# Which stream takes its turn first in a three-stage batch pipeline

## The chip, the cores and the metric

The kernel runs on one core of a Trainium2 chip. Times are device microseconds (us) of one execution. The core has a matrix engine (PE, with weight loads shown apart as PEld), a vector engine (DVE), an activation engine (ACT), a small-program engine (POOL) and a queue that issues DMA transfers (SP). Each engine works through its own instructions in the order in which they stand in its queue, and waits on semaphores for the others.

## The reference

Four graph layers run over x of shape (16, 1024, 128), 16 batches of 1024 nodes, with one 0/1 adjacency matrix of 1024 x 1024 for each batch. Every layer adds its result to x and norms each row. Layer 0 is a gated graph attention:

```
h = x @ W_w.T + W_b
e = einsum('bjl,bkl->bjk', h @ A, h);  e = e + swapaxes(e, 1, 2)
att = softmax(where(adj > 0, e, -9e15), axis=1) * adj
h_prime = relu(att @ h)
coeff = sigmoid(concat[x, h_prime] @ gate_w.T + gate_b)
x = layernorm(x + coeff * x + (1 - coeff) * h_prime)
```

Layer 1 thins the adjacency row after row (a sequential rule) and runs three graph convolutions with batch norms over all batches. Layer 2 is an attention of the same kind as layer 0 with three gates, a sigmoid and a tanh. Layer 3 is a graph convolution: two elus over x @ W0, then twice "multiply by a 128 x 128 matrix, propagate along the normed adjacency, add a bias", with an elu between, and the last residual and norm.

## The kernel before, in words

Nodes are tiled by 128, so a batch has NT = 8 tiles. The program has three stages that matter here: layer 0; layer 1 (thinning and convolutions); and layers 2 and 3 together. Layer 0 and layers 2 and 3 are each written as three Python generators over one batch, and the helper `in_turn` runs them as a pipeline.

`before(s, b)` prepares a batch. In layer 0 it loads x and eight adjacency blocks (L891, L895), casts each block on ACT (L897), tests it on DVE (L900), turns it on PE (L904) and stores it as fp8 (L905), and between them makes hT, G and hn, the attention's operands (L907 to L926). In layers 2 and 3 it loads the stored adjacency, three hidden matrices and x (L1208 to L1215), multiplies the hidden matrices by Wl (L765), adds, norms the rows, and makes hT, G and hn.

`attention(s, b)` goes over eight tiles and yields after each. For a tile it writes an additive mask on ACT (L939, L1554), multiplies the scores on PE (L723, in two halves of 512 columns), adds the mask and takes the row maximum on DVE (L942, L1559), takes the exponential on ACT (L946, L1563), forms scaled rows hs on DVE (L950, L1570) and accumulates on PE into `acc` (L953, L1573). The score tiles have two PSUM buffers and `acc` one.

`after(s, b)` ends a batch. It reads `acc` through a relu into hpT (L959, L1579), multiplies the gates on PE with 1 or 3 columns (L962, L1584), mixes x and h on DVE and norms the rows. In layers 2 and 3 the whole of layer 3 follows: turned rows x3T (L1613), the U0 product, two elus (L1481 to L1487), products with U1 and U2 (L1496), two propagations of 64 half-size matmuls in all (L1510), a last residual and norm, and the store of the output. Short PE products of all streams share two PSUM buffers with the tag `h`.

The row norm `normed` (L771 to L784) is the same everywhere: statistics on DVE (L777, L779), one add on DVE (L741), a power on POOL (L744), a product on DVE (L782) and eight scalings on ACT (L784). In the queue of DVE, L782 waits for POOL, and whatever stands behind it waits too.

What sets the order: `take_turns` steps through a list of streams and takes one yield from each in turn, and `in_turn` makes that list. The order of the Python calls is a priority. The framework's planner then fills each engine's queue: among the instructions whose inputs and buffers it expects to be free, it takes the one that was called first. So an engine's order is not the written order, and a turn that comes earlier in the list wins where two streams have something ready at once.

Of the kernel before, what the change touches and what calls it, by code (L numbers as in the profile page):

```python
# [639 lines left out]
def fast_kernel(ctx: ExitStack, tc: tile.TileContext, t: dict, out: bass.AP, flag: bass.AP):  # L640
# [45 lines left out]
    def nat(ap):  # L686
        return ap.rearrange("(t p) d -> p t d", p=P)
# [32 lines left out]
    def wide_matmul(psum, lhsT, rhs, tag="w"):  # L720
        p = psum.tile([P, N], F32, name="pmm", tag=tag)
        for h in range(H2):
            nc.tensor.matmul(p[:, h * 512:(h + 1) * 512], lhsT, rhs[:, h * 512:(h + 1) * 512],  # L723
                             start=True, stop=True)
        return p

    def tiles3(ap):
        return ap.rearrange("p (t d) -> p t d", d=P)

    def per_row(v):  # L730

        return v[:, :, None].to_broadcast([P, NT, P])
# [20 lines left out]
    def turned(psum, src, tag="h"):  # L753

        for p, c, blocks in halves(psum, tag):
            for i, k in enumerate(blocks):
                s = src[:, k, :] if len(src.shape) == 3 else src[:, k * P:(k + 1) * P]
                nc.tensor.transpose(p[:, i * P:(i + 1) * P], s, identf)  # L758
            yield p, c, slice(blocks[0], blocks[-1] + 1)
# [8 lines left out]
    def half_rows(v):  # L768

        return v[:, :, None].to_broadcast([P, 4, P])  # L770

    def normed(small, r):

        st = small.tile([P, NT, 6], F32, name="ln_st")
        mv = small.tile([P, NT, 2], F32, name="ln_mv")
        for i in range(NT):
            nc.vector.bn_stats(st[:, i, :], r[:, i, :])  # L777
        for i in range(NT):
            nc.vector.bn_aggr(mv[:, i, :], st[:, i, :])  # L779
        rstd = power_mhalf(small, mv[:, :, 1], add=LN_EPS, name="ln_rstd")  # L780
        nb = small.tile([P, NT], F32, name="ln_nb")
        nc.vector.scalar_tensor_tensor(nb, mv[:, :, 0], -1.0, rstd, op0=OP.mult, op1=OP.mult)  # L782
        for i in range(NT):
            nc.scalar.activation(r[:, i, :], r[:, i, :], AF.Identity, scale=rstd[:, i:i + 1], bias=nb[:, i:i + 1])  # L784
# [4 lines left out]
    def take_turns(streams):  # L789
        while streams:  # L790
            streams = [s for s in streams if next(s, streams) is not streams]

    def in_turn(before, attention, after, ahead=1, state=None):

        state = state or [Batch() for _ in range(B)]
        take_turns([before(state[b], b) for b in range(ahead)])
        for b in range(B - 1):
            streams = [attention(state[b], b)]  # L800
            if b:
                streams.append(after(state[b - 1], b - 1))
            if b + 1 >= ahead:
                streams.append(before(state[b + 1], b + 1))
            take_turns(streams)
        last, beside = attention(state[B - 1], B - 1), after(state[B - 2], B - 2)
        for i, _ in enumerate(last):
            if i % 2:
                next(beside, None)
        take_turns([beside, after(state[B - 1], B - 1)])  # L810
# [56 lines left out]
    with ExitStack() as ph:  # L867
# [62 lines left out]
        def attention(s, b):  # L930


            s.acc = ps_a.tile([P, N], F32, name="acc")
            for jt in range(NT):
                js = slice(jt * P, (jt + 1) * P)
                c = b * NT + jt
                mx = mx0[:, c:c + 1]
                msk = work.tile([P, N], BF16, name="msk", bufs=2)
                nc.scalar.activation(msk, Y[b][:, jt, :], AF.Identity, scale=BIG, bias=nbig)  # L939
                e = wide_matmul(ps_w, s.hT[:, js], s.G)  # L940
                em = work.tile([P, N], F32, name="em", bufs=2)
                nc.vector.tensor_tensor_reduce(em, e, msk, 1.0, -3.0e38, op0=OP.add, op1=OP.max, accum_out=mx)  # L942
                nmx = small.tile([P, 1], F32, name="nmx")
                nc.vector.tensor_scalar(nmx, mx, -1.0, None, op0=OP.mult)
                sm = small.tile([P, 1], F32, name="sm")
                nc.scalar.activation(em, em, AF.Exp, bias=nmx, accum_out=sm)  # L946
                rs = small.tile([P, 1], F32, name="rs")
                nc.vector.reciprocal(rs, sm)
                hs = small.tile([P, P], F32, name="hs")
                nc.vector.tensor_scalar(hs, s.hn[:, js], rs, None, op0=OP.mult)  # L950
                for h in range(H2):
                    c = slice(h * 512, (h + 1) * 512)
                    nc.tensor.matmul(s.acc[:, c], hs, em[:, c], start=(jt == 0), stop=(jt == NT - 1))  # L953
                yield

        def after(s, b):

            hpT = work.tile([P, N], F32, name="hpT")
            nc.scalar.activation(hpT, s.acc, AF.Relu)  # L959
            pz = ps_h.tile([P, NT], F32, name="pz", tag="h")  # L960
            for i in range(NT):
                nc.tensor.matmul(pz[:, i:i + 1], hpT[:, i * P:(i + 1) * P], gw[:, 1:2], start=True, stop=True)  # L962
            co = small.tile([P, NT], F32, name="co")
            nc.vector.tensor_add(co, pz, s.gx)
            nc.scalar.activation(co, co, AF.Tanh, scale=0.5, bias=gbh)
            cx = small.tile([P, NT], F32, name="cx")
            nc.vector.tensor_scalar(cx, co, 0.5, 1.5, op0=OP.mult, op1=OP.add)
            nc.vector.tensor_scalar(co, co, -0.5, 0.5, op0=OP.mult, op1=OP.add)
            yield
            r = work.tile([P, NT, P], F32, name="r")  # L970
            nc.vector.tensor_mul(s.xn, s.xn, per_row(cx))
            for p, c, k in turned(ps_h, hpT):
                nc.vector.tensor_mul(r[:, k, :], tiles3(p), half_rows(co[:, k]))
            nc.vector.tensor_add(s.xn, s.xn, r)
            yield
            normed(small, s.xn)
            nc.gpsimd.dma_start(nat(x1_d[b]), s.xn)
            yield

        in_turn(before, attention, after)  # L980


# [7 lines left out]
    with ExitStack() as ph:  # L990
# [171 lines left out]
        for i in range(len(steps) + 1):  # L1162
            streams = [fixed_point(*steps[i])] if i < len(steps) else []
# [58 lines left out]
    with ExitStack() as ph:  # L1222
# [194 lines left out]
        for l in range(3):  # L1417
# [9 lines left out]
            for i in range(B + lag[l]):  # L1427
                streams, left = left, []
# [31 lines left out]
    with ExitStack() as ph:  # L1460
# [115 lines left out]
        def after(s, b):  # L1576
# [64 lines left out]
            yield  # L1641

        in_turn(before, attention, after, 2, l2.state)
    l2.ctx.close()

# [45 lines left out]
```

## Time and profile before

| | us |
|---|---|
| median of 9 runs | 3121.43 |
| lowest and highest | 3108.71, 3126.36 |
| the profiled execution | 3126.31 |
| its span, from first to last instruction | 3124.6 |
| mean granted PE clock in it | 0.961 |
| first preparation of layer 0, alone | 0 to about 82 |
| layer 0, batches in the pipeline | 82 to 745 (PE busy 630.6, DVE 553.1, ACT 497.2) |
| thinning | 745 to about 1150 |
| convolutions of layer 1 and the first preparations of layer 2 | about 1150 to 1968 |
| layers 2 and 3, batches in the pipeline | 1968 to 3046 (PE busy 1008.3, DVE 738.0, ACT 698.4) |
| the last batch's end | 3046 to 3124.6 |

The profile is of one execution. Busy time is the union of an engine's instructions, and matmuls overlap at their ends. A row of a timeline has the start in us from the first instruction, the length, the engine, the line of the kernel, the operation, what it writes and reads, the shape, and how many equal instructions follow each other; brackets hold the idle time before it and what ended it. PE makes two passes over a 32-bit matmul, so one such matmul in the code is two in the profile. The granted clock is the share of PE's full clock that the chip let it have.

### The profile page before, as it was taken

How to read it: one execution, taken by the hardware profiler on the slowest of the kernel's cores; microseconds unless marked ns; L12 is line 12 of the kernel's file. 1: busy time of each engine (PE TensorE's matmuls, PEld its weight loads, DVE VectorE, ACT ScalarE, POOL GpSimd, SP SyncE). 2: the span in 40 equal slices, each digit the busy share in tenths (PEclk: the TensorE clock that was granted, in tenths of full speed). 3: DMA queues.
4: the chain of work that ended last, by engine and by line, in shares of the span. 5: the costliest groups of instructions: out<-in, count | busy, mean ns of one | idle time of the engine just before them, and what ended most of it. 6: DMA issues, size and time to landing. Idle time of an engine off the chain costs nothing.

```text
span 3124.6 us, 43145 instructions
## 1 busy us (share of the span) xinstructions
PE 2861.8 (92%) x15379; PEld 1846.8 (59%) x15442; DVE 2331.8 (75%) x5971; ACT 2017.5 (65%) x3393; POOL 326.8 (10%) x292
## 2 busy tenths in 40 slices
PE   7999999996899988999999987999999999999996
PEld 4454545453566655777788873555555555555554
DVE  7888888886999985666688785676666666766665
ACT  5777777774788775565555534666666666666653
POOL 0000000003000001111112231001000001100000
PEclk9999999998999999999999998999999999999997
DMA  5344434430000005223367692112111111111000
GB/s 173 130 138 149 136 132 145 145 125 29 1 2 2 2 25 211 82 95 122 122 220 247 220 346 74 35 61 68 65 57 54 62 67 55 54 55 54 21 14 22
DMA packets 123216, 297.98 MB, mean 95 GB/s; under 512 B 12656, under 2 KB 64624, under 8 KB 115824
## 3 DMA queue, kind: packets, MB, share of 16 engines
q1 hardware_dynamic: 102384, 211.13, 20.7%
q0 software_dynamic: 20608, 84.00, 7.1%
q8 instruction: 124, 2.03, 0.3%
q14 instruction: 100, 0.82, 0.1%
HBM read 211.04 MB, written 84.02 MB: 94 GB/s over the span
## 4 chain that ended last, share of the span: by engine, by line
PE 57%; DVE 22%; issue 5%; ACT 4%; POOL 4%; DMA 2%; POOLq 0%; SPq 0%; DVEq 0%; ACTq 0%
PE acc L1269 9%; PE ph L1510 7%; PE pmm L723 7%; PE acc L1573 5%; PE acc L953 4%; PE ph L765 4%; PE ph L758 4%; PE ph L1373 3%; PE s L1128 3%; POOL ln_rstd L744 3%; DVE ln_st L777 2%; PE ph L1496 2%; DVE mid L1082 2%; PE acc L1246 1%; DVE keep L1132 1%
## 5 line engine op out<-in xcount | busy, mean ns | idle before, releaser
L723 PE MATMUL pmm<-G,hT 128*128 128x512 f32 x1024 | 509.2, 619 | 6.8 <-DVE mx L942 3.4
L723 PEld LDWEIGHTS pmm<-G,hT 128*128 128x128 f32 x1024 | 186.3, 198 | 182.5 <-issue 138.9
L784 ACT ACTIVATE xn<-xn,ln_nb,ln_rstd 128x128 f32<-128x128 f32 x512 | 209.1, 481 | 121.2 <-DVE ln_nb L782 121.1
L1573 PE MATMUL acc<-em,hs 128*128 128x512 f32 x512 | 247.3, 598 | 22.1 <-DVE hs L1570 20.5
L953 PE MATMUL acc<-em,hs 128*128 128x512 f32 x512 | 254.3, 622 | 11.6 <-DVE hs L950 8.7
L744 POOL TENSOR_TENSOR ln_rstd<-ln_rstd,mhalf 128x8 f32<-128x8 f32 x64 | 117.0, 1828 | 1384.7 <-DVE ln_rstd L741 1063.3
L1269 PE MATMUL acc<-a,lo 128*128 128x512 f32 x768 | 241.1, 398 | 2.0 <-DVE lo L1237 2.0
L1269 PE MATMUL acc<-a,hi 128*128 128x512 f32 x768 | 242.1, 399 | 0.6 <-ACT a L1258 0.4
L1130 ACT ACTIVATE q<-s,negc 128x512 f16<-128x512 f32 x256 | 170.3, 693 | 66.9 <-issue 29.3
L1128 PE MATMUL s<-step,carry 128*128 128x384 bf16 (+3 forms) x1035 | 200.6, 305 | 7.3 <-DVE carry L1098 3.2
L1559 DVE CUSTOM_DVE_ANT_0 em<-pmm,msk 128x1024 f32<-128x1024 f32 x128 | 155.7, 1217 | 67.6 <-PE pmm L723 44.8
L1142 ACT ACTIVATE carry<-pc,negone 128x512 fp8e4<-128x512 f32 x256 | 166.4, 693 | 40.0 <-PE pc L1141 30.1
L939 ACT ACTIVATE msk<-carry,l0nbig 128x1024 bf16<-128x1024 fp8e4 x128 | 145.3, 1141 | 64.1 <-DVE mx L942 49.0
L900 DVE SCALAR_TENSOR_TENSOR chk<-an 128x1024 fp8e4<-128x1024 f32 x128 | 156.2, 1220 | 32.7 <-DMA an<-in_adj 31.8
L897 ACT ACTIVATE ab<-an 128x1024 bf16<-128x1024 f32 x128 | 134.6, 1052 | 69.9 <-PE pt L904 42.4
L942 DVE CUSTOM_DVE_ANT_0 em<-pmm,msk 128x1024 f32<-128x1024 f32 x128 | 155.6, 1215 | 24.6 <-PE acc L953 19.2
L1269 PEld LDWEIGHTS acc<-a,lo 128*128 128x128 f32 x768 | 142.8, 188 | 42.8 <-DVE lo L1237 9.5
L905 DVE TENSOR_SCALAR carry<-pt 128x1024 fp8e4<-128x1024 bf16 x128 | 155.2, 1217 | 16.4 <-PE pt L904 16.2
L953 PEld LDWEIGHTS acc<-em,hs 128*128 128x128 f32 x512 | 93.6, 196 | 122.4 <-issue 94.8
L1554 ACT ACTIVATE msk<-A,nbig 128x1024 bf16<-128x1024 fp8e4 x128 | 145.5, 1138 | 31.0 <-DVE mx L1559 28.7
L1573 PEld LDWEIGHTS acc<-em,hs 128*128 128x128 f32 x512 | 92.5, 190 | 117.1 <-issue 79.4
L1269 PEld LDWEIGHTS acc<-a,hi 128*128 128x128 f32 x768 | 141.6, 188 | 33.5 <-ACT a L1258 1.1
(278 smaller groups left out, 6601.4 us busy)
## 6 DMA issues: line engine op xcount, KB each, us to landing
an<-in_adj SPq DMA_DIRECT2D x128, 512.0 KB, 3.5
adj_d<-carry POOLq DMA_DIRECT2D x16, 1024.0 KB, 4.9
A<-dil_d SPq DMA_DIRECT2D x16, 1024.0 KB, 6.3
rdeg<-rdeg_d SPq DMA_DIRECT2D x32, 512.0 KB, 4.2
ag_d<-ag POOLq DMA_DIRECT2D x32, 512.0 KB, 5.3
ag<-ag_d SPq DMA_DIRECT2D x32, 512.0 KB, 6.2
A<-adj_d SPq DMA_DIRECT2D x16, 1024.0 KB, 4.9
xn<-in_x SPq DMA_DIRECT2D x16, 512.0 KB, 3.8
```

The lines of the kernel that those rows point to most:

```text
L723: nc.tensor.matmul(p[:, h * 512:(h + 1) * 512], lhsT, rhs[:, h * 512:(h + 1) * 512], start=True, stop=True)
L744: nc.gpsimd.tensor_tensor(r, r, mhalf[:, :n], op=OP.pow)
L784: nc.scalar.activation(r[:, i, :], r[:, i, :], AF.Identity, scale=rstd[:, i:i + 1], bias=nb[:, i:i + 1])
L900: nc.vector.scalar_tensor_tensor(chk, an, 0.0, an, op0=OP.is_gt, op1=OP.not_equal, accum_out=other[:, c:c + 1], saturate=False)
L953: nc.tensor.matmul(s.acc[:, c], hs, em[:, c], start=(jt == 0), stop=(jt == NT - 1))
L1128: nc.tensor.matmul(s[:, lo or 0:], y, twos if lo is None else step[:, :512 - lo], start=(j == 0), stop=(j == len(terms) - 1))
L1130: nc.scalar.activation(q[:, h * 512:(h + 1) * 512], s, AF.Abs, bias=st.negc[:, i:i + 1])
L1142: nc.scalar.activation(Y[b][:, hb, ks], pc, AF.Relu, bias=negone, saturate=False)
L1269: nc.tensor.matmul(acc, part[:, jt, :], pieces[h * NT // 2 + i][:, j, :], start=(jt == 0 and p == 0), stop=(jt == NT - 1 and p == 1))
L1510: nc.tensor.matmul(p, part[:, jt, :], A[:, jt, c], start=(jt == 0 and i == 0), stop=(jt == NT - 1 and i == 1))
L1559: nc.vector.tensor_tensor_reduce(em, e, msk, 1.0, 0.0, op0=OP.add, op1=OP.max, accum_out=mx)
L1573: nc.tensor.matmul(s.acc[:, c], hs, em[:, c], start=(jt == 0), stop=(jt == NT - 1))
```

## The change

`in_turn` makes its list of streams in another order. Before, the attention of batch b comes first, then the end of batch b - 1, then the preparation of the next batch. After, the end of batch b - 1 comes first, the attention of batch b second, the preparation third. The first round has no ending batch, and the last two steps after the loop are not touched. `in_turn` is called once in layer 0 (preparing one batch ahead) and once for layers 2 and 3 (two ahead).

```diff
         for b in range(B - 1):
-            streams = [attention(state[b], b)]
+            streams = []
             if b:
                 streams.append(after(state[b - 1], b - 1))
+            streams.append(attention(state[b], b))
             if b + 1 >= ahead:
                 streams.append(before(state[b + 1], b + 1))
             take_turns(streams)
```

## The prediction

> **What bounds the kernel now.** I read the totals first.
>
> ```profile
> PE 2861.8 (92%) x15379; PEld 1846.8 (59%) x15442; DVE 2331.8 (75%) x5971; ACT 2017.5 (65%) x3393; POOL 326.8 (10%) x292
> ```
>
> PE is nearly full on the mean, so only PE's gaps in the two stages that the edit touches can be won or lost. Layer 0 runs from 82 to 745 us, layers 2 and 3 from about 1968 to 3046. Next I took the engines' busy time batch by batch, a batch running from one gate matmul (L962 or L1584) to the next. Columns: window, its length, PE, PEld, DVE, ACT and POOL busy, granted clock, DMA share, GB/s. The first line is a batch of layer 0, the others are three successive batches of layers 2 and 3.
>
> ```profile
> 310.49:354.93 44.44, 41.12 (x189) 21.98 (x188) 38.52 (x93) 32.57 (x54) 3.16 (x3) 1.00 0.43 142
> 2178.31:2249.89 71.58, 66.60 (x267) 40.64 (x266) 50.63 (x156) 47.86 (x94) 6.75 (x4) 1.00 0.18 59
> 2249.89:2324.84 74.95, 69.96 (x267) 42.87 (x266) 50.63 (x156) 48.19 (x94) 6.75 (x4) 0.95 0.17 57
> 2324.84:2401.95 77.11, 72.53 (x267) 45.23 (x266) 50.67 (x156) 48.34 (x94) 6.75 (x4) 0.91 0.17 55
> ```
>
> At full clock a batch of layers 2 and 3 takes 71.6 us, with 5.0 us of PE gap each time; the longer batches are the same work under a lower clock. Where the 5.0 us are, the timeline of PE shows (start, length, instruction, in brackets the gap before and what ended it), in another full-clock batch, which starts at 2700.53:
>
> ```profile
> 2722.83 3.60 PE L723 MATMUL pmm<-G,hT 128*128 128x512 f32 x8
> 2728.01 1.12 PE L1573 MATMUL acc<-em,hs 128*128 128x512 f32 x2 [1.58 <-DVE hs L1570]
> ...
> 2732.24 1.88 PE L765 MATMUL ph<-x3T,U 128*128 128x512 f32 x4
> 2733.96 1.02 PE L723 MATMUL pmm<-G,hT 128*128 128x512 f32 x2
> 2737.90 2.22 PE L1496 MATMUL ph<-U,ehi 128*128 128x128 f32 x16 [2.92 <-DVE ehi L1483]
> ...
> 2741.00 0.63 PE L758 MATMUL ph<-identf,xn 128*128 128x128 f32 x4 [0.43 <-DVE zn L1498]
> ```
>
> The 2.92 us is the ending batch's elu chain (L1485 to L1483), with one half score tile (L723, 0.86 us) beside it. The 1.58 us is a DVE queue that stands behind a layer norm; DVE's and POOL's timelines:
>
> ```profile
> 2724.83 1.20 DVE L1526 TENSOR_TENSOR xn<-xn,yn 128x1024 f32<-128x1024 f32 x1
> 2727.59 0.17 DVE L782 SCALAR_TENSOR_TENSOR ln_nb<-ln_mv,ln_rstd 128x8 f32<-128x8 f32 x1 [1.55 <-POOL ln_rstd L744]
> 2727.67 0.28 DVE L1570 TENSOR_SCALAR hs<-hn,rs 128x128 f32<-128x128 f32 x1
> ```
>
> ```profile
> 2725.00 2.55 POOL L744 TENSOR_TENSOR ln_rstd<-ln_rstd,mhalf 128x8 f32<-128x8 f32 x1 [14.70 <-DVE rs L1568]
> 2731.45 1.64 POOL L744 TENSOR_TENSOR ln_rstd<-ln_rstd,mhalf 128x8 f32<-128x8 f32 x1 [3.90 <-DVE nmx L1561]
> ```
>
> In layer 0 PE's gaps are smaller and scattered, each a buffer or a scale that DVE hands over late:
>
> ```profile
> 326.14 1.98 PE L723 MATMUL pmm<-G,hT 128*128 128x512 f32 x4 [0.53 <-DVE mx L942]
> ...
> 333.47 1.95 PE L953 MATMUL acc<-em,hs 128*128 128x512 f32 x4 [0.92 <-DVE hs L950]
> ...
> 338.89 1.13 PE L765 MATMUL ph<-hT,l0As 128*128 128x512 f32 x2 [0.87 <-DVE carry L905]
> ```
>
> **The change, part by part.** No instruction is added or removed on any engine, and the three norm calls and every DMA stay. The turn decides which instruction the planner takes first when several are ready, so the edit acts in the 14 rounds with all three streams (b = 1 to 14), twice: 28 batches. The sums below follow the planned order of the changed kernel by hand: each queue in order, an instruction starting when its engine, its inputs and its buffer are there, durations from the rows. Times below count from the batch's first gate matmul.
>
> *Layers 2 and 3.* Full-size PE matmuls cost 0.43 us per pass, two passes for a half tile (0.86). PE work of a batch, passes times rows: scores, accumulations and projections 88 x 0.43 = 37.8; transposes 48 x 0.109 = 5.2; U products 32 x 0.1125 = 3.6; gates 3.6; propagation 64 x 0.2265 = 14.5; sum 64.8. Against 71.6, 6.8 us are lost: 4.9 in the three gaps, the rest in waits below a gap (0.58 and 0.55 inside runs of transposes).
>
> (a) *The 2.92 us.* In the new order an accumulation half and five score halves, 6 x 0.86 = 5.2 us, stand between the U0 product and L1496 (before: one). The chain gets longer, since an exp (1.15) now precedes the first elu on ACT and a masked maximum (L1559, 1.15) stands inside it on DVE: 3.9 becomes about 5.9. By the walk PE waits 0.5 for the first half and 0.3 for the second. 2.92 becomes 0.8.
>
> (b) *The 1.58 us* goes from that place, but DVE now runs the ending batch's output gate, its add and its norm statistics (L1597, L1598, L777, L779; 1.13 + 1.13 + 1.55 + 0.54 us, and 0.6 of L1525) ahead of tile 1's hs: hs is there at 20.6, PE could use it at 19.9. Cost 0.7.
>
> (c) *A new wait.* The transposes of the ending batch's normed rows now follow tile 1's accumulation, which ends at 22.35. The norm: statistics end 20.4, POOL 20.95 to 22.6, ACT's eight scalings (L784, 3.1 us in all) 22.75 to 25.85, copies, U0 at 27.1. PE has 0.88 of transposes, one score half and one accumulation half, 2.6 us, for these 4.75. Cost 2.15, where before the same stretch lost 0.58. Behind the waiting L782 on DVE stand tile 2's sm and hs; they come before PE asks for them.
>
> POOL's price in (c) is the one place where a rule chooses. The rows give 2.55 us beside L1526 and 1.64 beside other work. The Trainium skill's GPSIMD Engine Reference, Key points, says that POOL contends with VectorE instructions that have two SBUF inputs. L1526 is one; what now runs beside POOL is L1525, which reads PSUM. So I take 1.64; with 2.55 the stretch costs 0.9 more, 13 us over 14 batches.
>
> (d) The 0.43 us becomes about 0.3; nothing after the first propagation moves by more than 0.2. By the start of propagation the new order is at 40.2 us with 36.4 us of PE work done (3.8 lost), the old one at 40.85 with 34.7 (6.1 lost): the new order has one score half and one accumulation half more behind it. Gain 2.3 a batch; I take 2.0, since handovers of 0.05 to 0.1 us are not all in the walk. 14 x 2.0 = 28 us.
>
> *Layer 0.* PE work is 64 x 0.43 (27.5) + 8 x 0.43 (3.4) + 24 x 0.109 + 64 x 0.056 + 2 x 1.7 = 40.5 us; full-clock batches average 44.4. In the new order the vector work of the ending batch (L971 to L779, 1.13 + 1.2 + 1.13 + 1.55 + 0.54) stands ahead of tile 2's maximum on DVE. PE waits 0.4 for tile 0's hs, 1.15 for a score buffer, 0.75 for the next (its L942 stands behind L782, which waits for POOL) and 1.15 for tile 2's hs (its exp stands behind ACT's eight scalings): 3.5. The second half of the batch keeps PE fed. 40.5 + 3.5 + about 0.7 of handovers = 44.7: 0.3 worse, 14 x 0.3 = 4 us. Between -0.7 and +1.4 a batch is possible (-10 to +20 us), as DVE is busy for 38.5 of 44.4.
>
> *Queues.* On SP the load of x in layer 0 stands one adjacency block later, and in layers 2 and 3 the x rows follow the three h rows. Both wait for buffers that come free in the first third of a batch and are read over 40 us later: nothing, and if that cover went, one 512 KB load, 3.8 us by its row. POOL's order is the same.
>
> *The clock* is where a rule speaks against the change. Row: 1.00, 0.95, 0.91 above. Throttled stretches in the 15 batches sum to 78.5 us at half clock, 39 us lost, 2.6 a batch; they follow the narrow gate matmuls and, in one batch of three to five, the 2.92 us gap. The Trainium skill's TensorE: Matmul & The Clock Gate says (part 1) that an idle window of about 3.4 us halves the clock and (part 4) that transposes do not count as busy the same way. The stretch in (c) has from 22.35 to 25.4 only six transposes. By the rule it may be throttled in most batches, 3.4 to 6.8 us at half clock, 1.7 to 3.4 us each or 24 to 48 us; by the row, a 2.9 us gap was throttled rarely, and that gap goes. I take no change, -10 to +40.
>
> Sum: -28 + 4 + 0 = -24 us on the profiled execution (3126.3 us, span 3124.6), which stands 4.9 above the median; carried over, 3121.4 - 24 = 3097.
>
> **Rivals.** *The gains are taken back* (no difference): PE is at 92%, and if the waits in (b) and (c) are 2 us longer than walked, each batch is back at 71.6. For it: the gaps in my walk all hang on DVE and ACT queues that are crowded there. 3121. *The gate turns it slower*: the place is the wait in (c), the price 3.4 us a batch; it decides once it costs more than 2 us a batch, that is 4 us more at half clock. At 6.8 us throttled more in each batch: 14 x 3.4 = 48, so 3097 + 48 = 3145. *The gate helps*: without the 2.92 us gap its throttling goes (three batches with 13.65 us instead of 6.8 us, 3 x 3.4 = 10), and layer 0 gains 10 by the low end: 3121 - 28 - 10 - 10 = 3073. *The planner ignores turns*: excluded, the built order differs in all three stages.
>
> **Chances.** The walk 0.52; more gain 0.08; taken back 0.17; slower 0.23. A measurement here tells 0.3% (9 us) from nothing, so faster (under 3112) 0.60, same 0.17, slower 0.23. The likeliest case has 3080 to 3112 as its own range; for 8 in 10 I add the others' bounds to 3075 and 3142.
>
> **What would show it.** Right: full-clock batches of 69 to 70 us; L1496's gap under 1 us; L758 on xn, or a gap before it, taking 2 us more; POOL's first L744 after a gate near 1.64; layer 0 batches near 44.7. Wrong: a clock under 0.93 over the batches, or full-clock batches at 71 us or above.

## The result, and the profile after

| | us |
|---|---|
| kernel before, median of 31 runs (lowest, highest) | 3123.01 (3102.91, 3136.31) |
| changed kernel, median of 10 runs (lowest, highest) | 3095.41 (3090.45, 3104.86) |
| ratio, 95% interval | 0.9921 (0.9900 to 0.9942) |
| the profiled executions' spans | 3124.6 before, 3101.1 after |

The change makes the kernel 0.8% faster: 27.6 us between the medians, 23.5 us between the two profiled executions. The forecast was 3097. In the changed file every line behind `in_turn` has a number that is higher by one: L1496 is now L1497, L1573 is L1574, L942 is L943, while L723 to L784 keep theirs.

The engines' totals over the span (busy time, share, instructions), after:

```profile
PE 2860.9 (92%) x15379; PEld 1838.1 (59%) x15442; DVE 2328.8 (75%) x5971; ACT 2014.6 (65%) x3393; POOL 316.1 (10%) x292
```

The totals tell nothing of the gain: PE is busy for the same 2861 us. One has to go by stage. The two stages that the edit touches, each from its first to its last gate matmul, first of before, then of after (window, length, busy time of PE, PEld, DVE, ACT, POOL, granted clock, DMA share, GB/s):

```profile
85.83:746.36 660.53, 628.12 (x2762) 333.61 (x2760) 551.27 (x1340) 495.58 (x808) 67.67 (x45) 0.98 0.39 131
...
1968.09:3046.44 1078.35, 1008.62 (x3849) 615.97 (x3847) 737.95 (x2243) 698.29 (x1352) 95.23 (x57) 0.96 0.15 51
```

```profile
82.72:754.76 672.04, 624.35 (x2765) 333.89 (x2765) 556.24 (x1343) 496.53 (x809) 67.67 (x45) 0.99 0.39 129
...
1974.66:3022.30 1047.64, 1018.88 (x3852) 611.58 (x3850) 731.68 (x2248) 698.07 (x1355) 83.60 (x57) 0.96 0.16 53
```

Layers 2 and 3 are 30.7 us shorter, layer 0 is 11.5 us longer. The stretch before the first gate matmul is 3.1 shorter, the middle 1.8 shorter, the tail 0.6 longer: -3.1 + 11.5 - 1.8 - 30.7 + 0.6 = -23.5, the whole difference of the spans. That first stretch holds batch 0's attention too, not only the first preparation. The edit doesn't reorder its turns, and in the profiles here it ends anywhere between 82.7 and 86.4 us. Three batches after, one of layer 0 and two of layers 2 and 3:

```profile
361.04:406.24 45.20, 42.27 (x194) 22.88 (x193) 38.61 (x93) 34.36 (x57) 3.16 (x3) 1.00 0.42 140
...
2039.49:2109.90 70.41, 68.64 (x267) 41.14 (x266) 50.15 (x156) 47.90 (x94) 5.89 (x4) 0.98 0.19 60
...
2255.59:2327.57 71.98, 70.25 (x268) 42.07 (x266) 50.05 (x156) 48.00 (x94) 5.85 (x4) 0.95 0.18 59
```

PE's gap in a batch of layers 2 and 3 is 1.8 us where it was 5.0. In what follows, the "full-clock length" of a batch is its length less half of the time that the trace's clock records show at half clock (in layers 2 and 3 such stretches are 3.4 or 6.8 us long). Its median went from 71.5 to 68.6 us in layers 2 and 3 and from 44.4 to 45.2 in layer 0.

The place itself, on PE's timeline of the batch that starts at 2039.49 (start, length, instruction, in brackets the gap before it and what ended it):

```profile
2061.88 1.98 PE L1574 MATMUL acc<-em,hs 128*128 128x512 f32 x4 [0.81 <-DVE hs L1571]
2064.50 2.26 PE L758 MATMUL ph<-identf,xn 128*128 128x128 f32 x6 [0.64 <-ACT xn L784]
2066.59 1.02 PE L723 MATMUL pmm<-G,hT 128*128 128x512 f32 x2
...
2071.10 4.59 PE L723 MATMUL pmm<-G,hT 128*128 128x512 f32 x10
2075.53 2.26 PE L1497 MATMUL ph<-U,ehi 128*128 128x128 f32 x16
```

Ten passes of scores now stand in front of L1497, which finds its operand ready: the 2.92 us gap is gone. The 1.58 us in front of the accumulation is 0.81. A new gap of 0.64 stands in front of the turned rows. The six transposes after it hold PE for 2.09 us, until the next row starts, instead of 6 x 0.109 = 0.65: they start 0.385 us apart, as ACT's scalings do, since each waits for the next normed row. A wait is also 0.16 us longer than its shown gap, because a row runs past the moment when the next could start (a full-size matmul is 0.59 us long at a step of 0.43, a transpose 0.27 at 0.109). Summed over the stage, the groups of PE with their idle time before them (line, shape, count, busy time and mean ns, idle us and what ended it), first of before, then of after:

```profile
L1573 PE MATMUL acc<-em,hs 128*128 128x512 f32 x480 | 232.8, 598 | 22.1 <-DVE hs L1570 20.5 <-ACT elo L1481 1.6
...
L1496 PE MATMUL ph<-U,ehi 128*128 128x128 f32 x464 | 64.9, 296 | 38.0 <-DVE ehi L1483 38.0
...
L758 PE MATMUL ph<-identf,xn 128*128 128x128 f32 x232 | 44.3, 297 | 5.7 <-DVE zn L1498 4.4 <-ACT xn L784 0.3 <-DVE sm L1566 0.2
```

```profile
L1574 PE MATMUL acc<-em,hs 128*128 128x512 f32 x480 | 241.3, 612 | 12.1 <-DVE hs L1571 10.6 <-ACT elo L1482 1.6
...
L1497 PE MATMUL ph<-U,ehi 128*128 128x128 f32 x464 | 62.4, 281 | 0.2
L758 PE MATMUL ph<-identf,xn 128*128 128x128 f32 x232 | 53.4, 305 | 13.6 <-ACT xn L784 9.3 <-DVE zn L1499 0.4
```

38.0 became 0.2, 22.1 became 12.1, and 5.7 became 13.6. They repeat: the kernel before in a second profile (e7, below) has 38.0, 21.9 and 6.1, and three other kernels with the new order in this stage (e1, e3, e10) have 0.2, 12.1 and 13.6 or 13.7. In layer 0, PE's timeline of the batch that starts at 361.04 has the waits of the new order:

```profile
366.36 1.95 PE L954 MATMUL acc<-em,hs 128*128 128x512 f32 x4 [0.37 <-DVE hs L951]
...
372.08 0.61 PE L905 MATMUL pt<-identb,ab 128*128 128x128 bf16 x8 [0.23 <-ACT xT L910]
373.29 1.98 PE L723 MATMUL pmm<-G,hT 128*128 128x512 f32 x4 [0.60 <-DVE mx L943]
...
376.59 1.98 PE L723 MATMUL pmm<-G,hT 128*128 128x512 f32 x4 [0.46 <-DVE mx L943]
...
380.69 3.67 PE L954 MATMUL acc<-em,hs 128*128 128x512 f32 x8 [1.25 <-DVE hs L951]
```

### The profile page after: what moved, and what is told of

It reads as the page before. It is cut to its first block, busy times and chain, and to the rows that moved or that the text cites. A ratio compares the mean times of both kernels' runs of the same rounds, so it can differ in the third digit from the quotient of the medians.

```text
span 3101.1 us, 43140 instructions
## 1 busy us (share of the span) xinstructions
PE 2860.9 (92%) x15379; PEld 1838.1 (59%) x15442; DVE 2328.8 (75%) x5971; ACT 2014.6 (65%) x3393; POOL 316.1 (10%) x292
## 4 chain that ended last, share of the span: by engine, by line
PE 64%; DVE 20%; issue 6%; ACT 5%; POOL 3%; DMA 3%; SPq 0%; POOLq 0%; DVEq 0%; ACTq 0%
PE pmm L723 10%; PE acc L1270 9%; PE ph L1511 7%; PE ph L765 6%; PE acc L1574 5%; PE acc L954 5%; PE ph L758 4%; PE ph L1374 4%; PE s L1129 2%; PE ph L1497 2%; DVE mid L1083 2%; POOL ln_rstd L744 2%; PE acc L1247 2%; ACT xn L784 2%; DVE ln_st L777 2%
## 5 line engine op out<-in xcount | busy, mean ns | idle before, releaser
L723 PE MATMUL pmm<-G,hT 128*128 128x512 f32 x1024 | 521.4, 626 | 19.2 <-DVE mx L943 16.5
L723 PEld LDWEIGHTS pmm<-G,hT 128*128 128x128 f32 x1024 | 182.0, 198 | 182.5 <-issue 113.0
L1574 PE MATMUL acc<-em,hs 128*128 128x512 f32 x512 | 255.8, 611 | 12.1 <-DVE hs L1571 10.6
L784 ACT ACTIVATE xn<-xn,ln_nb,ln_rstd 128x128 f32<-128x128 f32 x512 | 206.5, 481 | 80.4 <-DVE ln_nb L782 80.3
L744 POOL TENSOR_TENSOR ln_rstd<-ln_rstd,mhalf 128x8 f32<-128x8 f32 x64 | 105.4, 1646 | 1297.9 <-DVE ln_rstd L741 1240.4
L954 PEld LDWEIGHTS acc<-em,hs 128*128 128x128 f32 x512 | 94.3, 192 | 144.3 <-issue 107.4
L1555 ACT ACTIVATE msk<-A,nbig 128x1024 bf16<-128x1024 fp8e4 x128 | 146.0, 1141 | 48.4 <-DVE mx L1560 46.4
L906 DVE TENSOR_SCALAR carry<-pt 128x1024 fp8e4<-128x1024 bf16 x128 | 155.9, 1220 | 21.0 <-PE pt L905 20.5
L943 DVE CUSTOM_DVE_ANT_0 em<-pmm,msk 128x1024 f32<-128x1024 f32 x128 | 155.4, 1214 | 7.1 <-PE acc L954 5.1
L947 ACT ACTIVATE em<-em,nmx 128x1024 f32<-128x1024 f32 x128 | 145.9, 1140 | 21.1 <-DVE nmx L945 17.7
```

The source lines that it names most:

```text
L744: nc.gpsimd.tensor_tensor(r, r, mhalf[:, :n], op=OP.pow)
```

## The experiments

Where an experiment changes turns, `in_turn` gets an argument that gives the order for each of its two calls: t is the attention of batch b, e the end of batch b - 1, p the preparation. "tep" is the kernel before, "etp" the change. Each ratio is against runs of the kernel before on the same chip. No kernel leaves work out.

**One half of the change at a time (e1, e2).**

```diff
-    def in_turn(before, attention, after, ahead=1, state=None):
+    def in_turn(before, attention, after, ahead=1, state=None, turns="tep"):
-            streams = [attention(state[b], b)]
+            ready = {"t": attention(state[b], b)}
             if b:
-                streams.append(after(state[b - 1], b - 1))
+                ready["e"] = after(state[b - 1], b - 1)
             if b + 1 >= ahead:
-                streams.append(before(state[b + 1], b + 1))
+                ready["p"] = before(state[b + 1], b + 1)
+            streams = [ready[w] for w in turns if w in ready]
 # e1: layers 2 and 3
-        in_turn(before, attention, after, 2, l2.state)
+        in_turn(before, attention, after, 2, l2.state, turns="etp")
 # e2: layer 0 instead
-        in_turn(before, attention, after)
+        in_turn(before, attention, after, turns="etp")
```

> Only layers 2 and 3 take the new turns, layer 0 keeps the old ones. Theory (the stages add up): layers 2 and 3 gave 30.9 us (1078.4 to 1047.6 between first and last gate matmul) and layer 0 took 8 us of it back, so this kernel stands about 8 us below the changed one: 3087, ratio to the kernel before 0.988 to 0.990. Rival (layer 0's loss was chance, or was paid back by the higher clock it had): 3095, ratio 0.992. Full-clock batches of layers 2 and 3 near 68.6 us, of layer 0 near 44.4.

Measured: 3088.56 us (3083.26 to 3100.05), ratio 0.9900 (0.9864 to 0.9936).

> Only layer 0 takes the new turns. Theory: slower, since a batch of layer 0 at full clock takes 45.2 us in place of 44.4, 14 x 0.8 = 11 us, less up to 7 us of throttling that went: 3127 to 3134, ratio 1.001 to 1.004, and layers 2 and 3 back at 71.6 us a batch. Rival (layer 0 did not lose anything): 3123 or less, ratio 1.000 or below.

Measured: 3117.62 us (3097.50 to 3123.81, 14 runs), ratio 0.9985 (0.9959 to 1.0010). The stages of e1 (first pair, layer 0 and layers 2 and 3) and of e2 (second pair), columns as above:

```profile
83.23:744.66 661.43, 628.01 (x2762) 333.76 (x2761) 551.12 (x1340) 495.57 (x808) 67.67 (x45) 0.98 0.38 131
...
1962.52:3011.26 1048.74, 1020.62 (x3852) 613.81 (x3850) 731.57 (x2248) 698.08 (x1355) 83.61 (x57) 0.96 0.16 53
```

```profile
83.24:749.56 666.32, 620.49 (x2765) 332.84 (x2766) 555.34 (x1343) 497.13 (x809) 67.68 (x45) 1.00 0.38 130
...
1969.43:3037.27 1067.84, 996.97 (x3850) 607.13 (x3848) 737.84 (x2244) 697.42 (x1352) 95.24 (x57) 0.98 0.16 52
```

e1 has all the gain and no loss: 1048.7 us in layers 2 and 3, as in the changed kernel, and the old 661 in layer 0. Its median is 6.9 us under the changed kernel's, as the theory had it, though the intervals of the two ratios overlap. e2 has layer 0's full-clock batch of 45.2 us, as the changed kernel, but not the expected loss: its median lies in the rival's range. In its profile layer 0 lost only 5.8 us, since 3.4 us instead of 23.9 were at half clock there, and layers 2 and 3, whose program is the old one, were 10.5 us shorter at the clock 0.98 instead of 0.96. That asked whether the clock belongs to the kernel or to the execution.

**The same two kernels again (e6, e7).** e6 is e2's program, e7 the unchanged kernel before, each run once, with a profile.

> The same kernel as in e2 (new turns in layer 0 alone), looked at a second time. If the lower clock loss of e2's layers 2 and 3 (51.2 us throttled, against 78.5 before) belongs to the kernel, that is to where its gate matmuls and gaps fall in the throttle's windows, it comes again within 7 us; if the windows fall by chance in each execution, it lies anywhere between 50 and 90 us.

> The kernel before, unchanged, looked at a second time, to see how far the throttled time of one kernel differs between executions: near 23.9 us in layer 0 and 78.5 us in layers 2 and 3 if it belongs to the kernel; anywhere between 3 and 24 us and between 50 and 90 us if it is chance.

Measured, with the half-clock time summed from the trace's clock records:

| execution | time | layer 0: length, at half clock | layers 2 and 3: length, at half clock |
|---|---|---|---|
| before | 3126.31 | 660.5, 23.9 | 1078.4, 78.5 |
| before again (e7) | 3112.53 | 659.3, 20.5 | 1066.3, 51.2 |
| layer 0 alone (e2) | 3117.21 | 666.3, 3.4 | 1067.8, 51.2 |
| layer 0 alone again (e6) | 3133.92 | 667.2, 0 | 1081.9, 85.3 |

Layer 0's figures come again: 6 to 8 us lost by the new order. Its half-clock time is 0 to 10 us with the new order (10.2 in the changed kernel) and 17 to 24 with the old one (23.9 in e1, 17.1 in e4), so that difference goes with the program. In layers 2 and 3 the same program had 51.2 us at half clock once and 78.5 or 85.3 the other time: that is the execution's, and it moves the total by 14 to 17 us.

The clock records show what differs between two executions. In layers 2 and 3 every half-clock stretch begins on a grid with steps of 3.413 us, to within 0.01 us, and the grid lies elsewhere in each execution. Of the 60 batches of this table in layers 2 and 3, all whose first gate matmul stands 1.05 to 1.33 us behind a step of the grid have 6.8 us of half clock that begins within 5 us, all at 1.34 to 1.78 have none, and all at 2.64 to 3.17 have 3.4. A full-clock batch of 71.6 us is just short of 21 steps (71.68), so the gates slip back by about 0.1 us a batch or less. In the first profile of before the second batch stands at 1.54 and the fifth is the first under 1.33; in e7 the second stands at 1.78 and the ninth is the first under 1.33. The Trainium skill's TensorE: Matmul & The Clock Gate (part 1) says that the gate's windows run freely and don't reset with a kernel; the grid agrees.

e2's median tells neither way with certainty: it can't be told from no change, but its interval ends at 1.0010, 3 us, so a loss of 6 to 8 us in the whole kernel lies just outside. The loss stands in the stage itself, in both profiles; what gave it back in e2's 14 runs is not shown.

**Other orders in layer 0 (e3, e10).** Both keep "etp" in layers 2 and 3.

```diff
 # e3
-        in_turn(before, attention, after)
+        in_turn(before, attention, after, turns="tpe")
 # e10
-        in_turn(before, attention, after)
+        in_turn(before, attention, after, turns="pte")
```

> Layers 2 and 3 with the new turns; layer 0 with attention first, preparation second, the ending batch last. Theory (in layer 0 it is the ending batch's vector chain and norm standing ahead of the attention's row maxima on DVE that costs PE): with the chain behind them PE's waits for hs and for score buffers shrink, layer 0 batches at 43.5 to 44.4 us, total 3075 to 3087. Rival (layer 0 loses with any order but the old one): batches at 45 us or more, 3095 or more.

Measured: 3059.56 us (3053.21 to 3063.67), ratio 0.9806 (0.9771 to 0.9840). This is the fastest kernel of the study: 1.9% under the kernel before, 36 us under the changed one, and below the theory's range, in time as in its batches.

> Layer 0 with preparation, attention, ending; layers 2 and 3 as in e3. DVE theory (PE waits in layer 0 for row maxima and scaled rows, so whatever vector work is called ahead of the attention costs PE time): the preparation's 16 passes of 1.2 us on DVE now go ahead of the maxima, full-clock batches of 43.5 to 45.5 us instead of e3's 42.6, so 3059.6 + 14 x 1.9 = 3086 us (3072 to 3100). Rival (only the ending's vector work does harm, because its norm makes DVE stand still for POOL; preparation never waits for POOL): batches of 42.8 us or less, 3057 to 3063 us.

Measured: 3090.68 us (3085.83 to 3096.25), ratio 0.9915 (0.9886 to 0.9945). Full-clock batches of layer 0 have a median of 44.8 us, against 42.6 in e3: both measures lie in the range of the DVE theory, and the rival is out. A layer 0 batch of e3, then the two groups of PE that wait for DVE in layer 0, for the changed kernel, e3 and e10 in this order:

```profile
253.54:296.22 42.68, 41.87 (x193) 22.65 (x193) 38.27 (x93) 34.19 (x57) 3.16 (x3) 1.00 0.44 148
```

```profile
L723 PE MATMUL pmm<-G,hT 128*128 128x512 f32 x468 | 237.0, 610 | 15.7 <-DVE mx L943 15.2
L954 PE MATMUL acc<-em,hs 128*128 128x512 f32 x480 | 227.4, 610 | 24.9 <-DVE hs L951 24.8
```

```profile
L723 PE MATMUL pmm<-G,hT 128*128 128x512 f32 x468 | 231.9, 603 | 0.0
L954 PE MATMUL acc<-em,hs 128*128 128x512 f32 x477 | 225.3, 600 | 6.0 <-DVE rs L949 5.5 <-DVE hs L951 0.4
```

```profile
L723 PE MATMUL pmm<-G,hT 128*128 128x512 f32 x471 | 233.6, 613 | 11.8 <-DVE mx L943 11.7
L954 PE MATMUL acc<-em,hs 128*128 128x512 f32 x480 | 232.6, 612 | 9.2 <-DVE hs L951 7.2 <-DVE nmx L945 0.9 <-ACT hpT L960 0.9
```

The two waits sum to 40.6, 6.0 and 21.0 us. The order decides whose vector work stands in front of a row maximum or a scaled row on DVE. With the ending or the preparation ahead of the attention PE waits; with the attention first and the ending last it hardly does. The old order also has the attention first, but the ending second; its two groups wait 2.7 and 10.4 us, and a further 17.1 us lie in front of its turned blocks, projections and gate products (3.4, 7.5 and 6.2, most of them waiting for L905 or ACT), where e3 has 1.6. Only the order of ending and preparation differs between the two, so the 1.8 us a batch come from that swap. Why the swap also took layer 0's half-clock time to zero was not tried by itself.

**The same two other orders in layers 2 and 3 (e4, e9).**

```diff
 # e4, layer 0 as before
-        in_turn(before, attention, after, 2, l2.state)
+        in_turn(before, attention, after, 2, l2.state, turns="ept")
 # e9, layer 0 as in e3
-        in_turn(before, attention, after, 2, l2.state)
+        in_turn(before, attention, after, 2, l2.state, turns="tpe")
```

> Layer 0 old; layers 2 and 3 with the ending batch first, the preparation second, the attention last. The planned order has 2 score halves (1.7 us) between the U0 product and L1496, where the changed kernel has five and an accumulation half (5.2 us). Theory (the gain is the cover of the elu chain by score products): PE's gap before L1496 is 2 to 3 us again, full-clock batches at 70.5 to 71.6 us, total 3110 to 3123. Rival (the gain is that the ending batch goes first, whatever stands behind it): batches at 68.6 us, total 3087.

Measured: 3152.09 us (3150.68 to 3153.69), ratio 1.0103 (1.0057 to 1.0148), slower than before.

> Attention, preparation, ending in layer 0 (as in e3) and in layers 2 and 3 too, where e3 has the ending first. Cover theory (in layers 2 and 3 the ending is a long chain through ACT, DVE and POOL, and it must start early so that scores and accumulations are left to cover its waits): with the ending last its first rows come later, the gaps in front of the turned rows, of L1497 and of the first propagation come back at 5 us or more a batch, full-clock batches of 72 us or more instead of 68.6: 3059.6 + 14 x 3.5 = 3109 us or more. Rival (the ending is better last everywhere, as layer 0 has shown, since its vector work then never stands ahead of a row maximum): full-clock batches of 67.5 us or less, 3044 us or less.

Measured: 3091.37 us (3088.21 to 3098.12), ratio 0.9915 (0.9884 to 0.9946), 32 us slower than e3. The groups of PE over layers 2 and 3, first e4, then e9:

```profile
L723 PE MATMUL pmm<-G,hT 128*128 128x512 f32 x477 | 239.5, 626 | 17.9 <-DVE mx L1560 17.9
...
L1497 PE MATMUL ph<-U,ehi 128*128 128x128 f32 x464 | 58.7, 278 | 11.4 <-DVE ehi L1484 11.4
L758 PE MATMUL ph<-identf,xn 128*128 128x128 f32 x232 | 55.9, 345 | 48.3 <-ACT xn L784 47.2
```

```profile
L1574 PE MATMUL acc<-em,hs 128*128 128x512 f32 x480 | 253.6, 636 | 23.2 <-DVE hs L1571 17.3 <-ACT elo L1482 3.3 <-DVE ln_rstd L741 1.1
...
L1497 PE MATMUL ph<-U,ehi 128*128 128x128 f32 x464 | 60.1, 279 | 4.6 <-DVE ehi L1484 4.6
L758 PE MATMUL ph<-identf,xn 128*128 128x128 f32 x232 | 45.6, 304 | 31.2 <-ACT xn L784 17.5 <-ACT xT L1533 8.1 <-DVE ehi L1488 4.4
```

In both the wait is back, mostly not in front of L1497, where the theory had put it, but one step earlier in the ending's chain, in front of the transposes of the normed rows (47.2 and 17.5 us). So the size of the loss in e4 was under-forecast (3110 to 3123), and its place was half missed. Its full-clock batches alternate between about 64 and 79 us, where one length was forecast (the mean of the 13 middle ones, 71.2, lies in the forecast range), so e4 differs from the changed kernel by more than the waits named. In e9 the full-clock batches alternate between about 72.5 and 67 to 68.5 us; the 13 middle ones average 70.2, against 68.8 in e3. The stage is 35.7 us longer than e3's: 22 in full-clock lengths, and 14 from 27 us more at half clock. Both measures lie between what the two theories said: the ending last is not better everywhere, and it costs less than the cover theory forecast.

**Taking the DVE wait for POOL away (e5, e8).** The 1.58 us and parts of (c) rest on L782, where DVE waits for POOL's power with the rest of its queue behind it. In e5 (the kernel before otherwise) and e8 (the turns of e3) DVE doesn't wait:

```diff
-        nc.vector.scalar_tensor_tensor(nb, mv[:, :, 0], -1.0, rstd, op0=OP.mult, op1=OP.mult)
+        nc.vector.tensor_scalar(nb, mv[:, :, 0], -1.0, None, op0=OP.mult)
+        nc.gpsimd.tensor_tensor(nb, nb, rstd, op=OP.mult)
```

> The kernel before with its old turns in all layers; only the norm is changed: the product mean x rstd that L782 takes on DVE (which waits there for POOL's power) becomes a negation on DVE that needs no POOL result, and a product on POOL behind the power. Queue theory (the 1.58 us gap in front of L1573 and part of layer 0's gaps are DVE queues that stand behind a waiting L782): full-clock batches of layers 2 and 3 lose the 1.58 us gap and come to 70.0 us, the 2.92 us gap in front of L1496 stays, layer 0's batches come to about 44.0; 15 x 1.5 + 14 x 0.4 = 28 us, so 3093 us. Rival (the gap is the chain of the rows' own sums, and the queue behind L782 hides it): no change within 6 us. Rival (the norm's own chain grows by POOL's second operation, about 0.5 to 1.6 us, and the ending batch is what PE waits for): 3130 us or more, with a longer gap in front of the x3T products.

Measured: 3154.68 us (3148.88 to 3159.12), ratio 1.0116 (1.0085 to 1.0147). The groups over layers 2 and 3, then the timelines of POOL, DVE and PE in the batch that starts at 2332.41:

```profile
L1574 PE MATMUL acc<-em,hs 128*128 128x512 f32 x480 | 247.6, 626 | 1.4 <-ACT elo L1482 1.3
...
L1497 PE MATMUL ph<-U,ehi 128*128 128x128 f32 x464 | 64.3, 289 | 26.2 <-DVE ehi L1484 26.2
L758 PE MATMUL ph<-identf,xn 128*128 128x128 f32 x232 | 59.1, 331 | 33.3 <-ACT xn L785 28.9 <-DVE sm L1567 0.7
```

```profile
2360.15 2.63 POOL L744 TENSOR_TENSOR ln_rstd<-ln_rstd,mhalf 128x8 f32<-128x8 f32 x1 [17.97 <-DVE ln_nb L782]
2362.85 0.20 POOL L783 TENSOR_TENSOR ln_nb<-ln_nb,ln_rstd 128x8 f32<-128x8 f32 x1
```

```profile
2363.39 0.25 DVE L1571 TENSOR_SCALAR hs<-hn,rs 128x128 f32<-128x128 f32 x1
```

```profile
2363.64 3.17 PE L758 MATMUL ph<-identf,xn 128*128 128x128 f32 x8 [1.99 <-ACT xn L785]
2366.59 1.91 PE L1574 MATMUL acc<-em,hs 128*128 128x512 f32 x2
```

The 20.5 us that accumulations waited for hs are gone to the last tenth, but not because hs comes earlier. It starts 31.0 us after the gate here, 27.6 without what the half clock costs in that stretch, and 27.1 in the kernel before (2727.67 - 2700.53). The planner put another norm's statistics ahead of it on DVE, and on PE it put eight transposes of normed rows, behind a gap of 1.99 us, ahead of tile 1's accumulation; in the kernel before that accumulation came first and three transposes after it. So e5 does not test the queue theory, whose 3093 it missed. PE now stands in front of the turned rows (28.9 us where before had 0.3), the full-clock batch is 71.3 instead of 71.5, and 136.5 us of the stage are at half clock instead of 51 to 79. The second rival was right in sign and place, though POOL's extra product takes only 0.2 us in most norms and 0.8 in some.

> Both edits together: layer 0 with the ending batch last, layers 2 and 3 with the ending batch first (the kernel of e3), and the norm's product on POOL as in e5. Queue theory: of the gaps that stay in layers 2 and 3, the 0.8 us in front of tile 1's accumulation (behind the ending batch's own vector work, not behind L782) stays and the wait for the turned rows grows by POOL's second operation, so layers 2 and 3 gain at most 0.3 us a batch or lose up to 0.7; layer 0 gains 0.3 a batch where a maximum stood behind L782. Sum between -9 and +6 us on e3's 3059.6: about 3057 us. Rival (gains of turns and of the product add): 28 us less than e3, 3032 us.

Measured: 3152.40 us (3145.18 to 3156.39), ratio 1.0112 (1.0082 to 1.0142). Both forecasts were far off. The planner laid layers 2 and 3 out anew, in alternating batches of two lengths:

```profile
2241.70:2311.40 69.70, 65.23 (x250) 41.42 (x248) 43.74 (x124) 40.48 (x79) 4.73 (x4) 0.90 0.13 41
2311.40:2395.90 84.50, 77.59 (x284) 44.59 (x283) 57.08 (x186) 55.84 (x109) 10.69 (x10) 0.96 0.20 66
```

A longer batch takes over work of its neighbour (284 matmuls against 250). 29.5 us are spent in front of the turned rows and 24.6 in front of scores. Since one added instruction moves so much of the order, e5 and e8 show where waits stand in these two layouts, but neither tests nor prices the wait at L782 by itself. What sets the alternation stays open.

## Why the prediction was right

**(a), the 2.92 us: right in mechanism, mis-sized.** It was to become 0.8 and became 0; 38.0 us of idle time in front of L1496 are 0.2 after. The score halves cover the elu chain entirely. It takes the attention ahead of the preparation for that, as e4 shows: with the ending first and the attention third, 11.4 us are back there and 47.2 one step earlier (in batches that are laid out otherwise as well).

**(b), the 1.58 us: right.** 0.7 was walked; 0.81 is shown as a gap, 0.97 with the 0.16. The cause is the one named: hs (L1571) stands on DVE right behind the ending's statistics. That the old gap was the queue behind L782 stands in the rows of before: rs, the last input of hs, was there at 2724.91, and hs started at 2727.67, right behind the waiting L782. DVE before, then after:

```profile
2724.76 0.15 DVE L1568 RECIPROCAL rs<-sm 128x1 f32<-128x1 f32 x1
```

```profile
2061.02 0.63 DVE L779 BATCH_NORM_AGGREGATE ln_mv<-ln_st 128x2 f32<-128x6 f32 x8
2061.56 0.26 DVE L1571 TENSOR_SCALAR hs<-hn,rs 128x128 f32<-128x128 f32 x1
```

**(c), the new wait: right.** 2.15 us were walked. The profile has it in two pieces: the gap, 0.64 as shown and 0.80 with the 0.16, and 2.09 - 0.65 = 1.44 inside a run of six transposes, together 2.24. A reader who counts only gaps would miss about two thirds of it. The choice of POOL's price was right too, by this batch's timelines of POOL and of DVE:

```profile
2062.06 1.65 POOL L744 TENSOR_TENSOR ln_rstd<-ln_rstd,mhalf 128x8 f32<-128x8 f32 x1 [10.81 <-DVE ln_rstd L741]
```

```profile
2061.80 0.69 DVE L1526 TENSOR_TENSOR yn<-ph,mf 128x512 f32<-128x512 f32 x1
2063.75 0.17 DVE L782 SCALAR_TENSOR_TENSOR ln_nb<-ln_mv,ln_rstd 128x8 f32<-128x8 f32 x1 [1.25 <-POOL ln_rstd L744]
```

The power took 1.65 us here, beside an instruction of DVE that reads PSUM for 0.4 us and beside an idle DVE for the rest. The whole stage gives the fuller comparison. In before, the 13 powers beside L1526 (an add of two SBUF tiles, 1.03 us of overlap) all took 2.55, and the 15 beside the masked maximum L1559, which reads PSUM (1.1 us of overlap), 1.64 to 1.65, as beside an idle DVE. In the batch of e5 above it took 2.63 again, with L1527, the same add, beside it. This agrees with the rule of the Trainium skill's GPSIMD Engine Reference (Key points).

**The sum of layers 2 and 3.** 2.3 a batch was walked, 2.0 taken, 2.9 measured (71.5 to 68.6). The walk's own waits, 0.8 + 0.7 + 2.15 + 0.3, sum to 3.95 and not to 3.8, so it stood for 2.1 to 2.3. (a) brings 0.8 more than walked and (d) nearly 0.3 (of 4.4 us in front of L758 on xn that DVE's zn ended, 0.4 are left in the whole stage); (b) and (c) take 0.3 and 0.1 back. That makes 2.8 to 3.0; the 0.3 that I had taken off for handovers was not needed. Over the stage the full-clock lengths fall by 34.1 us, the half-clock time takes 3.4 of it back, and 30.7 stay; the forecast was 28.

**Layer 0: right in sign, mis-sized.** The failing term is "+0.3 a batch": it is +0.8. The four waits that the walk named all came (gaps of 0.37, 0.60, 0.46 and 1.25, for the 0.4, 1.15, 0.75 and 1.15 walked); with 0.16 added to each they sum to 3.3, for the 3.5 walked. The walk left out a fifth, 0.23 + 0.16 = 0.4 in front of turned adjacency blocks, and its "about 0.7 of handovers" was too small: 45.2 less 40.5 of PE work less 3.7 of waits leaves 1.0. Over the stage the full-clock lengths rise by 18.4 us, since some rounds lose more (the second and third batch have 46.4 and 47.3 us for 44.5 and 43.9, the last but one 47.1 for 42.5), and 6.9 us come back through 13.7 us less at half clock: 11.5 where 4 was forecast, inside its bounds of -10 to +20. e1 says the same by time: without layer 0's part the kernel is 6.9 us faster. e2's median does not.

**The clock: the sum was about right, by two errors that nearly cancel.** "No change" hid one loss and one gain. Of the batches of layers 2 and 3, the table counts those with a half-clock stretch that begins 15 to 34 us after the gate, and those with one that begins later. (c) lies 24.4 to 27.1 us after the gate, the old 2.92 us gap 34.4 to 37.4:

| kernel | idle before the transposes of normed rows, ended by ACT | 15 to 34 us: batches of 15, us | after 34 us: batches, us |
|---|---|---|---|
| before | 0.3 | 0, 0 | 3, 20.5 |
| before again (e7) | 0.3 | 1, 3.4 | 2, 13.7 |
| after | 9.3 | 8, 30.7 | 0, 0 |
| all ending last (e9) | 17.5 | 11, 37.5 | 1, 3.4 |
| old turns, product on POOL (e5) | 28.9 | 14, 58.0 | 3, 10.2 |
| ending, preparation, attention (e4) | 47.2 | 14, 68.3 | 0, 0 |

What the rule that spoke against the change (TensorE: Matmul & The Clock Gate, parts 1 and 4) had forecast came at the place that I had named, in 8 of 15 batches, at 15 us lost, below the 24 to 48. Whether the wait or the transposes bring it is not separated. The row's side came true as well: the 20.5 us of the old gap went, as the rival "the gate helps" had it. The three other kernels with the new order in this stage (e1, e3, e10) have 9.3 us of that wait too and 6 to 8 batches. Over the table, the longer PE stands in front of these transposes, the more batches are at half clock there. These are orders that differ in other ways too, so the table shows that the two go together, not a price.

Of the rivals, none came: the gains were not taken back, since (b) and (c) cost what the walk said, to within 0.3 us, and (c)'s half-clock time came to 30.7 / 15 = 2.0 us a batch, half of the 4 from which it would have decided. Its mechanism is real, though: e4 and e5 are slower than the kernel before, and 41 and 58 us more at half clock in layers 2 and 3 than in the first profile of before are part of that.

That 3097 came within 2 us of 3095.41 is partly luck: -28 was 2.7 too weak, +4 was 7.5 too weak the other way, and start, middle and tail gave 4.3 that nobody forecast.

## What to carry to other kernels

Where a planner fills the queues, the order of the streams is a priority, and the right one is a matter of the stage: here the ending paid when put first where its long chain through other engines had PE work to lie beside it (layers 2 and 3), and when put last where its vector work only stood in front of what PE waits for (layer 0). Four of the six orders were run in each stage. Try each stage by itself, since a change in one shared helper added a gain of 31 us to a loss of 6 to 12 here, and the best pair that was tried was worth 1.9%. And count a wait that is spread inside a run of short instructions by the run's length against its usual price, not only by the gaps that a view lists.

## What the hardware showed that was not expected

- One program, the kernel before, had 78.5 us of layers 2 and 3 at half clock in one execution and 51.2 in another (e2's program 51.2 and 85.3), which moves its time by 14 to 17 us. The half-clock stretches begin on a grid of 3.413 us, and how far the first gate of a batch stands behind a step of it told in all 60 batches of four executions how much half clock followed. Single profiles of two kernels can't be compared below that without taking the clock out.
- POOL's power on 128 x 8 values took 1.64 to 1.65 us beside an idle DVE or one that reads PSUM for 1.1 us of it, and 2.55 beside an add with two SBUF inputs that overlaps it for 1.03 us.
- Taking away a wait of DVE for POOL, with a small product moved from DVE to POOL, made the kernel 1.2% slower (e5), in an order that the planner had laid out anew: the full-clock batches were even 0.2 us shorter, but 58 to 85 us more of layers 2 and 3 than in the two profiles of before were at half clock.
